# Cross-attention on one Trainium2 core: the softmax sum of half 0 taken from right sums of products 1 and 2, T1 of e and T4 of y made by ScalarE and transfers

## The chip, the core and the metric

The kernel runs on one core of a Trainium2 chip. The core's engines work side by side, each through its own list of instructions in order: TensorE (PE in the profile, its weight loads PEld) multiplies matrices out of the on-chip memory into accumulation banks; VectorE (DVE), ScalarE (ACT) and GpSimd (POOL) work element by element; SyncE (SP) issues plain transfers. GpSimd also issues transfers, among them those that add what they bring to what already stands at the destination. The engines wait for each other by semaphores.

The metric is the device time of one execution in microseconds (us). Unless another unit is named, all times below are us.

## The reference

Eight batches, each with a query source x1 and a context x2 of 512 channels by 1024 positions:

```python
B, C1, C2, N = (8, 512, 512, 1024)          # D = C2 // 8 = 64
q = jnp.einsum('bcn,dc->bnd', x1, Wq) + bq
k = jnp.einsum('bcn,dc->bdn', x2, Wk) + bk[:, None]
v = jnp.einsum('bcn,dc->bdn', x2, Wv) + bv[:, None]
attn = jax.nn.softmax(jnp.einsum('bnd,bdm->bnm', q, k), axis=2)
attn_out = jnp.einsum('bcm,bnm->bcn', v, attn)
return attn_out + x1
```

All of it is in 32-bit floats.

## The kernel before, in words

**Order of the mathematics.** For each batch the kernel computes scores with keys on the partitions and queries along the free dimension, subtracts each query's maximum, and takes exponentials: this is e. Then it multiplies the context itself with e (y = x2 · e), divides y by the sum of the exponentials over the keys, and only then applies Wv, the bias and x1 (o = Wv · y + bv + x1).

**Halves and blocks.** Queries are taken in two halves h = 0 and 1 of H = 512 columns; keys in two halves of four tiles of 128 (MH = 4). So e is a 2 x 2 matrix of blocks: "11" and "21" are the two key halves for queries of half 0, "12" and "22" those of half 1. x2 (called a) and Wv (called w) are 2 x 2 blocks too.

**Seven products.** Both multiplications use a scheme of seven block products instead of eight. For y its right sums are T1 = e12 − e11, T2 = T1 + e22, T3 = e22 + e12 and T4 = T2 − e21 with its sign turned where the code says so; its left sums are S1 to S4 of a. Most of the seven products of y are split in the same way once more: `left_stream` and `right_stream` make the inner S and T sums of product i (tiles aI and eI with the product's number), `multiply_seeded` runs the inner products in the order 1, 7, 6, 2, 5, 4, 3. There, ScalarE copies a partial result out of a running chain of accumulation (L746) while TensorE works on something else, and TensorE then goes on in the same chain. The products of o use `multiply_41` (with y's product 4), `multiply` and `multiply_57`; their T1, T2 and T4 of y are made in `sum_y`.

**Periods.** `period(s, n, nn, nnn)` runs once per batch. It holds the products of y and o of batch s, and beside them the scores, maxima, exponentials and first sums of batch n, the next one; nn and nnn are those behind it. The order of all instructions on every engine is the order in which the functions are called: nothing reorders them. `s.six` holds for batches 2 to 5, `five` is true in the periods of batches 1 to 6. Batch 0, batch 1 and the last one have branches of their own.

**Queues.** ScalarE's list holds in one order the exponentials (L331), the copies of the scores (L245), the copies out of the chains (L746, L849), evictions of outputs (L930) and copies with the sign turned (L165, L177, L355). POOL's list holds the reductions across partitions (maximum L272, sum L291) and the issues of all transfers that add: x1 into outputs (L942, L900), a's sums (L160, L169, L181), T3 of e (L366, e22 into e12), T4 of e (L361), and tiles of e into the softmax sum (`add_tile`, L966). These transfers share one queue and move in its order. Plain loads and the outputs go by SP's queue.

**The softmax sum of half 0 of batch n.** In period s: `first_sum` copies tile 0 of e to a tile of sums (ScalarE, L971) and adds tile 1 by a transfer; tiles 2 and 3 are added by two more transfers, each issued when its exponential is made (`add_exponential`, `add_tile`). At the end of the period `total` adds the two key halves on VectorE (L266), and `reduce_total` adds across partitions on POOL and moves the result to a small tile of 128 x 4 (`few`). `invert` takes the reciprocals and writes them to a row in DRAM; `spread` broadcasts that row. For half 1 the sum comes from T3 (`sum_1`), since T3 is e12 + e22.

**T1, T2, T3 of e of batch n.** After its last exponential, `open_t` names the tiles, VectorE makes T1 (L340, two instructions, one for each pair of tiles), and two transfers make T3 in the place of e12. At the start of the next period, behind product 1, VectorE makes T2 = T1 + e22 (L340 again). Product 6 needs T2, product 5 needs T1 (its inner right sums are `sums_5`, L537 eI5), products 7 and 3 come behind.

**T4 of y** is y21 − T2, made by VectorE (L429), read by the last product of o in the period (`second(4)`, L464 ps_oc<-yT,w).

Of the kernel before, what the change touches and what calls it, by code (L numbers as in the profile page):

```python
# [15 lines left out]
def kernel(  # L16
# [48 lines left out]
    P = 128  # L65
# [211 lines left out]

    def sum_1(s):

        t = s.t["T3"]  # L280
        s.mx[1] = sb.tile([P, 2, H], F32, tag="fold", name=f"sum_{s.b}_1", bufs=2)
        nc.vector.tensor_tensor(s.mx[1], t[:, 0:2, :], t[:, 2:4, :], ALU.add)
        fold_halves(s, 1, ALU.add)
# [53 lines left out]
    def right_sums(t, k):  # L337

        x, y = {"T1": ("12", "11"), "T2": ("T1", "22"), "T3": ("22", "12")}[k]
        nc.vector.tensor_tensor(t[k], t[x], t[y], ALU.subtract if k == "T1" else ALU.add)  # L340
# [173 lines left out]

    def left_stream(s, i, x, tag):

        v = {f"{p + 1}{q + 1}": x[:, ts(q, MH // 2), ts(p, P)] for p in range(2) for q in range(2)}
        sums = sb.tile([P, 4, MH // 2, P], F32, tag=tag, name=f"aI{i}_{s.b}")
        s.inner[i] = v
        for z, (k, x, y, op) in enumerate(LEFT):  # L520
            v[k] = sums[:, z]
            nc.vector.tensor_tensor(v[k], v[x], v[y], op)  # L522
            yield
# [4 lines left out]
    def right_stream(s, i, x, *tags):  # L528
# [5 lines left out]
        sums = [sb.tile(shape, F32, tag=t, name=f"eI{i}{t}_{s.b}") for t in tags]  # L534
        both, t2, t4 = sums[0][:, 0:2], sums[-1][:, last - 2], sums[-1][:, last - 1]
# [577 lines left out]
    def period(s, n, nn, nnn):  # L1113
# [42 lines left out]
        def add_exponential(i):  # L1156
            exponential(n, 0, i)
            add_tile(n, 0, i)

        def while_11(j):  # L1160
            if five and j == 0 and nn:
                add_exponential(3)

        def while_57(j):
            if nn:
                exponential(n, 1, j)
            elif j == 0:
                add_exponential(3)
            else:
                exponential(n, 1, 0)  # L1170
# [4 lines left out]

        def first_sum():
            copy_first(n, 0)
            add_tile(n, 0, 1)
# [56 lines left out]
        else:  # L1235
# [3 lines left out]
            sum_e(s, *(("T2",) if early else ("T1", "T2")))  # L1239
# [14 lines left out]
            if n and not early:  # L1254
                invert(s, 0)
            if s.b > 1:
# [103 lines left out]
        if n:  # L1360
# [15 lines left out]
            elif nn:  # L1376
                first_sum()
# [28 lines left out]
        if five:  # L1406
# [4 lines left out]
            next(products, None)  # L1411
            if s.six:
                exponential(n, 0, 2)
            if nn is None:
                first_sum()
# [13 lines left out]
        scale_y(s, "21")  # L1429
        if n is None:  # L1430
# [28 lines left out]
        if s.six:  # L1459
            add_tile(n, 0, 2)  # L1460
        elif five:
            add_exponential(2)
# [13 lines left out]
        if n:  # L1476
            if five:
                sums_1 = left_stream(n, 1, n.a["11"], "i2")
                next(sums_1)
                weave(sums_1, singly(lambda: lower(n, 1, 2), lambda: sum_y(s, "T4")))  # L1480
# [38 lines left out]
        if n:  # L1519
# [14 lines left out]
            total(n, 0)  # L1534
# [46 lines left out]
```

## Time and profile before

| | us |
|---|---|
| median of 3 runs | 665.4 (664.44 to 666.31) |
| span of the profiled execution, first to last instruction | 662.5 |
| TensorE busy in it | 657.7 |
| VectorE busy | 622.4 |
| ScalarE busy | 379.7 |
| GpSimd busy | 225.5 |
| share of the 16 transfer engines taken by POOL's queue, SP's queue | 50.4%, 30.6% |

The profiled execution is one execution on the chip; of it the profile gives the span and not the time of the whole execution, which takes in what lies ahead of the first and behind the last instruction. The granted clock of TensorE is 1.000 over the span.

In a timeline, a line gives the start, the duration, the engine, the source line, the operation, out<-in by the program's names, the shapes, and how many instructions are merged; in brackets stands how long the engine had been idle and what ended it. Matmuls overlap: one of 128x256 lasts 0.38 in the records, though the next starts 0.216 after it. Each matmul of the source is two instructions in the trace. A line of transfer issues gives the size of one transfer and the time from issue to landing. A line of a queue gives packets, MB, and the share of the engines' time in the stretch that was asked for.

### The profile page before, as it was taken

Reading aid. Unit: us, or ns where it says so; the run is one execution under the profiler, and the core shown is the slowest. Engines: PE = TensorE matmul, PEld = TensorE weight load, DVE = VectorE, ACT = ScalarE, POOL = GpSimd, SP = SyncE. Lnnn points to the kernel's source line nnn. Section 1 sums busy time; section 2 is a strip of 40 time slices with the busy share of each in tenths; the row PEclk is TensorE's granted clock in tenths of the full one; section 3 lists DMA queues with packets and bytes.
Section 4 is the critical chain, followed back from the end, with each engine's and each line's share of the span. In section 5 each row is a group of like instructions: output and inputs, shape, how many; then the busy total and the mean of one; then the engine's idle time right before and its main releaser. Section 6 shows DMA issues by size and latency. Waiting matters only on the chain.

```text
span 662.5 us, 7988 instructions
## 1 busy us (share of the span) xinstructions
PE 657.7 (99%) x2626; PEld 433.7 (65%) x2626; DVE 622.4 (94%) x869; ACT 379.7 (57%) x728; POOL 225.5 (34%) x192
## 2 busy tenths in 40 slices
PE   9999999999999999999999999999999999999997
PEld 4435755756658666677666686576865757666865
DVE  1999999999999998999989999899999989999997
ACT  3755557446475575665756647656576555574332
POOL 0125215631255412463126431364213640244300
PEclk9999999999999999999999999999999999999999
DMA  8688578994899859998599995998948994399604
GB/s 329 259 281 255 118 256 147 210 261 142 276 162 227 240 164 299 194 245 198 166 290 204 227 232 148 276 209 203 273 91 192 216 243 176 77 180 242 132 15 152
DMA packets 51545, 135.88 MB, mean 205 GB/s; under 512 B 5680, under 2 KB 6192, under 8 KB 51504
## 3 DMA queue, kind: packets, MB, share of 16 engines
q0 software_dynamic: 24512, 61.94, 50.4%
q1 hardware_dynamic: 26848, 73.29, 30.6%
q8 instruction: 21, 0.34, 0.2%
q10 hardware_dynamic: 144, 0.14, 0.1%
q14 instruction: 20, 0.16, 0.1%
HBM read 87.83 MB, written 16.81 MB: 158 GB/s over the span
## 4 chain that ended last, share of the span: by engine, by line
PE 98%; DMA 1%; SPq 0%; DVE 0%; issue 0%
PE ps_yc L555 9%; PE ps_ya L555 7%; PE ps_oc L464 7%; PE ps_oa L689 7%; PE ps_s L236 6%; PE ps_ya L464 4%; PE ps_oa L464 4%; PE ps_q L191 4%; PE ps_i5chain L555 3%; PE ps_i4b L840 3%; PE ps_k L191 3%; PE ps_i3chain L555 3%; PE ps_i7chain L555 3%; PE ps_oc L840 3%; PE ps_i1chain L555 3%; PE ps_i2chain L555 3%
## 5 line engine op out<-in xcount | busy, mean ns | idle before, releaser
L331 ACT ACTIVATE e<-e 128x1024 f32<-128x1024 f32 x60 | 63.4, 1059 | 25.6 <-DVE e L322 25.2
L291 POOL PARTITION_ALL_REDUCE den<-sum x16 | 52.8, 3298 | 59.0 <-DVE sum L266 54.2
L322 DVE TENSOR_TENSOR e<-e,top 128x1024 f32<-128x1024 f32 x60 | 72.3, 1217 | 0.2 <-POOL top L272 0.2
L272 POOL PARTITION_ALL_REDUCE top<-max x16 | 31.4, 1960 | 94.1 <-DVE max L266 68.1
L966 POOL DMA_DIRECT2D sum<-e x21 | 25.9, 1235 | 82.0 <-ACT sum L971 32.6
L245 ACT COPY e<-ps_s 128x512 f32<-128x512 f32 x90 | 47.8, 622 | 10.1 <-PE ps_s L236 7.6
L236 PE MATMUL ps_s<-q,k 64*128 64x512 f32 (+1 forms) x188 | 46.6, 598 | 0.0
L256 DVE TENSOR_TENSOR max<-max,e 128x1024 f32<-128x1024 f32 x30 | 36.6, 1218 | 0.3
L236 PEld LDWEIGHTS ps_s<-q,k 64*128 64x128 f32 x188 | 17.5, 186 | 19.9 <-issue 17.4
L875 DVE TENSOR_TENSOR y<-y,den 128x1024 f32<-128x1024 f32 x24 | 29.2, 1220 | 0.3
L522 DVE TENSOR_TENSOR aI<-a,aI 128x256 f32<-128x256 f32 x60 | 28.1, 468 | 0.9
L746 ACT COPY ps_yc<-ps_i7chain 128x256 f32<-128x256 f32 x32 | 11.4, 357 | 30.2 <-PE ps_i7chain L555 26.1
L689 PE MATMUL ps_oa<-yT,w_S 128*128 128x512 f32 x56 | 27.4, 592 | 0.0
L307 POOL DMA_DIRECT2D den<-row x12 | 6.7, 558 | 59.0 <-DMA row<-few 47.8
L522 DVE TENSOR_TENSOR aI<-a 128x256 f32<-128x256 f32 x60 | 26.3, 464 | 0.0
L689 PE MATMUL ps_oa<-y,w_S 128*128 128x512 f32 x56 | 26.3, 592 | 0.0
L191 PE MATMUL ps_q<-x_in_x_dram,wqk_sb 128*64 128x512 f32 x112 | 25.6, 598 | 0.0
L746 ACT COPY ps_ya<-ps_i5chain 128x256 f32<-128x256 f32 x32 | 11.5, 361 | 24.2 <-PE ps_i5chain L555 20.0
L464 PE MATMUL ps_oa<-yT,w_S 128*128 128x512 f32 x56 | 25.2, 593 | 0.0
L464 PE MATMUL ps_oc<-yT,w 128*128 128x512 f32 x56 | 25.2, 592 | 0.0
L555 PE MATMUL ps_yc<-e,aI 128*128 128x256 f32 x92 | 23.6, 379 | 0.0
L746 ACT COPY ps_ya<-ps_i1chain 128x256 f32<-128x256 f32 x28 | 10.0, 357 | 22.1 <-PE ps_i1chain L555 18.5
(346 smaller groups left out, 1840.0 us busy)
## 6 DMA issues: line engine op xcount, KB each, us to landing
x_in_x_dram<-in_x_dram SPq DMA_DIRECT2D x60, 512.0 KB, 7.9
a<-in_x2T_dram SPq DMA_DIRECT2D x32, 512.0 KB, 7.0
aS<-in_x2T_dram POOLq DMA_DIRECT2D x21, 512.0 KB, 10.2
sum<-e POOLq DMA_DIRECT2D x21, 512.0 KB, 6.2
eT<-eT POOLq DMA_DIRECT2D x16, 512.0 KB, 11.9
r<-in_x_dram POOLq DMA_DIRECT2D x14, 512.0 KB, 8.3
uo<-in_x_dram POOLq DMA_DIRECT2D x14, 512.0 KB, 9.8
out_dram<-r SPq DMA_DIRECT2D x14, 512.0 KB, 8.9
```

Source lines behind the costliest of these rows:

```text
L191: nc.tensor.matmul(ps[r, :], w_sb[:, c, :], s.x[:, c, ts(h, H)], start=(c == 0), stop=(c == CT - 1),)
L236: nc.tensor.matmul(ps[g][:, n], s.k[r, ts(i, P)], s.q[r, ts(h, H)][:, n], start=True, stop=True)
L245: nc.scalar.copy(e[:, g, i, :], ps[g])
L256: nc.vector.tensor_tensor(f, e[:, :, 0, :] if i == 1 else f, e[:, :, i, :], op)
L291: nc.gpsimd.partition_all_reduce(s.den[h], s.mx[h][:, 0, :], P, ReduceOp.add)
L322: nc.vector.tensor_tensor(e, e, top, ALU.subtract)
L331: nc.scalar.activation(e, e, AF.Exp)
L464: nc.tensor.matmul(ps, left[ka][:, k, ts(j, P)], right[kb][:, k, :], start=opens and k == 0, stop=i in (2, 3, 4) and k == n_k - 1, skip_gr ...
L522: nc.vector.tensor_tensor(v[k], v[x], v[y], op)
L555: nc.tensor.matmul(ps, s.inner[i][ka][:, k, :], s.inner[i, "t"][kb][:, k, :], start=opens and k == 0, stop=z in (2, 3, 4) and k == n_k - 1 ...
L689: nc.tensor.matmul(ps, w[ka][:, k, ts(j, P)], s.y[kb][:, k, :], start=False, stop=i == 3 and k == 1, skip_group_check=True,)
L840: nc.tensor.matmul(ps, s.inner[i][ka][:, k, :], s.inner[i, "t"][kb][:, k, :], start=opens and k == 0, stop=z in (2, 3, 4) and k == n_k - 1 ...
```

## The change

Three edits, with what follows from them in the order of calls.

1. **Half-0 sum of batches 2 to 7.** The copy and the three transfers of the sum are dropped; the exponentials keep their places. The inner right sums of products 1 and 2 are made with another set of signs, so that their T3 is e22 + e12 of the inner blocks and T4 + T3 is e21 + e11; the left sums of these two products turn sign to match (`LEFT_SUM`). In `right_stream` a single 128x1024 instruction for T1 and T3 becomes two of 128x512. `total_0` adds the pairs T4, T3 of both products in one 128x1024 instruction, whose output is laid out so that after the reduction a small tile of 64 x 8 holds, for every four queries, both parts. `invert` adds the parts for the left queries before the reciprocal.
2. **T1 of e, batches 2 to 5.** VectorE no longer makes T1. ScalarE writes −e22 to its tile in two halves (`begin_t1`, behind the issues of T3). In the next period VectorE makes T2 as T3 − e11, and two transfers add T2 to the tile of T1 (`end_t1`, ahead of S4's transfer on POOL).
3. **T4 of y, in the periods of batches 1 to 5.** ScalarE writes −T2 to its tile behind the copies of `multiply_41` (`copy_yt4`), and a transfer adds y21 to it once that is scaled. The VectorE instruction is dropped.

```diff
+    def total_0(s):
+        s.mx[0] = f = sb.tile([P, 2, H], F32, tag="fold", name=f"sum_{s.b}_0", bufs=2)
+        x, y = (s.inner[i, "m"].rearrange("q z k (p f) -> q z k p f", p=D) for i in (1, 2))
+        nc.vector.tensor_tensor(f.rearrange("q k (p z f) -> q z k p f", p=D, z=2), x, y, ALU.add)
+        fold_halves(s, 0, ALU.add)
+        s.den[0] = sb.tile([P, H], F32, tag="den", name=f"den_{s.b}_0", bufs=2)
+        nc.gpsimd.partition_all_reduce(s.den[0], f[:, 0, :], P, ReduceOp.add)
+        s.few[0] = sb.tile([D, 2, H // P], F32, tag="fews", name=f"fews_{s.b}", bufs=2)
+        nc.gpsimd.dma_start(
+            s.few[0].rearrange("p z f -> p (z f)"), s.den[0][0:1, :].rearrange("o (p f) -> o p f", p=D)
+        )
...
     def invert(s, h):
-        nc.vector.reciprocal(s.few[h], s.few[h])
+        few = s.few[h]
         s.row[h] = row = dram.tile([1, H], F32, tag="row", name=f"row_{s.b}_{h}")
-        nc.gpsimd.dma_start(row.rearrange("o (p f) -> (o p) f", p=P), s.few[h])
+        to = row.rearrange("o (p f) -> (o p) f", p=P)
+        if h == 0 and s.b > 1:
+            nc.vector.tensor_tensor(few[:, 0, :], few[:, 0, :], few[:, 1, :], ALU.add)
+            to = row.rearrange("o (z p f) -> (o p) z f", z=2, p=D)
+        nc.vector.reciprocal(few, few)
+        nc.gpsimd.dma_start(to, few)
...
+            "T2 of T3": ("T3", "11", ALU.subtract),
...
+    def begin_t1(s):
+        for i in (0, 2):
+            nc.scalar.mul(s.t["T1"][:, i : i + 2, :], s.t["22"][:, i : i + 2, :], -1.0)
+
+    def end_t1(s):
+        for i in (0, 2):
+            nc.gpsimd.dma_start(
+                s.t["T1"][:, i : i + 2, :], s.t["T2"][:, i : i + 2, :], accum_op=ALU.add
+            )
...
+    def copy_yt4(s):
+        nc.scalar.mul(s.y["T4"], s.y["T2"], -1.0)
...
-        for z, (k, x, y, op) in enumerate(LEFT):
+        for z, (k, x, y, op) in enumerate(LEFT_SUM if i in (1, 2) else LEFT):
...
+        if i in (1, 2):
+            for z, k in enumerate(("T1", "T2", "T4", "T3")):
+                v[k] = sums[z // last][:, z % last]
+            s.inner[i, "t"], s.inner[i, "m"] = v, sums[-1][:, last - 2 : last]
+            for k, x, y, op in (
+                ("T1", "12", "11", ALU.subtract),
+                ("T3", "22", "12", ALU.add),
+                ("T2", "T1", "22", ALU.add),
+                ("T4", "21", "T2", ALU.subtract),
+            ):
+                nc.vector.tensor_tensor(v[k], v[x], v[y], op)
+                yield
+            return
...
         def while_11(j):
             if five and j == 0 and nn:
-                add_exponential(3)
+                exponential(n, 0, 3)
...
-            sum_e(s, *(("T2",) if early else ("T1", "T2")))
+            sum_e(s, *(("T2 of T3",) if s.six else ("T2",) if early else ("T1", "T2")))
...
+            if s.six:
+                end_t1(s)
             if s.b > 1:
                 add_s4(s)
...
-            elif nn:
-                first_sum()
...
+            if nn:
+                copy_yt4(s)
             if s.six:
                 exponential(n, 0, 2)
...
         scale_y(s, "21")
+        if five and nn:
+            nc.gpsimd.dma_start(s.y["T4"], s.y["21"], accum_op=ALU.add)
...
-        if s.six:
-            add_tile(n, 0, 2)
-        elif five:
-            add_exponential(2)
+        if five and not s.six:
+            exponential(n, 0, 2)
...
             if nn:
-                sum_e(n, "T1")
+                if not n.six:
+                    sum_e(n, "T1")
                 sum_t3(n, 0)
                 sum_t3(n, 2)
+                if n.six:
+                    begin_t1(n)
...
-            total(n, 0)
+            if five:
+                total_0(n)
+            else:
+                total(n, 0)
```

More of the change, by code (lines that the diff above doesn't have):

```diff
@@ L337, in right_sums @@
     def right_sums(t, k):
-        x, y = {"T1": ("12", "11"), "T2": ("T1", "22"), "T3": ("22", "12")}[k]
-        nc.vector.tensor_tensor(t[k], t[x], t[y], ALU.subtract if k == "T1" else ALU.add)
+        x, y, op = {
+            "T1": ("12", "11", ALU.subtract),
+            "T2": ("T1", "22", ALU.add),
+            "T3": ("22", "12", ALU.add),
+            "T2 of T3": ("T3", "11", ALU.subtract),
+        }[k]
+        nc.vector.tensor_tensor(t[k[:2]], t[x], t[y], op)
     def open_t(s):
@@ L513, in in_turn @@
             yield from stream
+    LEFT_SUM = (
+        ("S3", "21", "11", ALU.subtract),
+        ("S1", "21", "22", ALU.subtract),
+        ("S2", "11", "S1", ALU.subtract),
+        ("S4", "12", "S2", ALU.subtract),
+    )
     def left_stream(s, i, x, tag):
@@ L1154, in scores_0 @@
             return then
-        def add_exponential(i):
-            exponential(n, 0, i)
-            add_tile(n, 0, i)
         def while_11(j):
             if five and j == 0 and nn:
-                add_exponential(3)
+                exponential(n, 0, 3)
         def while_57(j):
@@ L1167, in while_57 @@
             elif j == 0:
-                add_exponential(3)
+                exponential(n, 0, 3)
             else:
@@ L1174, in early_s2 @@
             add_11(n, "S2")
-        def first_sum():
-            copy_first(n, 0)
-            add_tile(n, 0, 1)
         if not s.t:
@@ L1414, in period @@
             if nn is None:
-                first_sum()
                 begin_s1(n)
@@ L1479, in period @@
                 next(sums_1)
-                weave(sums_1, singly(lambda: lower(n, 1, 2), lambda: sum_y(s, "T4")))
+                weave(
+                    sums_1, singly(lambda: lower(n, 1, 2), *([] if nn else [lambda: sum_y(s, "T4")]))
+                )
         if n is None:
```

## The prediction

> **What bounds the kernel now.** I read the busy times on the first page, then the waits of TensorE, then the order of time around the places that the change touches.
>
> ```profile
> PE 657.7 (99%) x2626; PEld 433.7 (65%) x2626; DVE 622.4 (94%) x869; ACT 379.7 (57%) x728; POOL 225.5 (34%) x192
> ```
>
> All waits of TensorE in the trace are two, both in the head:
>
> ```profile
> PE ps_warm L1029 <- DVE warm L1026: 1.0, 1, 1.0
> PE ps_ka L1003 <- DMA x_head<-in_x2h_dram: 0.3, 1, 0.3
> ```
>
> The span is TensorE's own work, matmul behind matmul, and the change touches no matmul. VectorE, which it relieves in some batches, is 94% busy and still never late by a wait that shows. So time saved on VectorE has nothing to shorten; what can change the time is a hand-off to TensorE that comes later than now. The rest is a search for those, in a period of the middle batches (here the change from batch 2 to batch 3; batches 2 to 5 have the same order).
>
> **ScalarE at the start of a batch.** ScalarE gets the two copies that begin T1 (−"22", 128x1024 each). They stand in its queue behind the last exponential, and ahead of the eviction of output "12" (L930), the negation for S3 (L177) and the copies of product 1. The rows of ScalarE, of TensorE beside it, and of the VectorE instruction that releases the exponential:
>
> ```profile
> 272.09 1.22 DVE L322 TENSOR_TENSOR e<-e,top 128x1024 f32<-128x1024 f32 x1
> 273.34 1.06 ACT L331 ACTIVATE e<-e 128x1024 f32<-128x1024 f32 x1 [1.59 <-DVE e L322]
> 274.31 1.25 ACT L930 ACTIVATE r<-ps_oa,wqk_sb 128x512 f32<-128x512 f32 x2
> 275.44 1.05 ACT L177 ACTIVATE a<-a 128x1024 f32<-128x1024 f32 x1
> 276.57 1.03 PE L555 MATMUL ps_i1chain<-e,a 128*128 128x256 f32 x4
> 277.69 0.36 ACT L746 COPY ps_ya<-ps_i1chain 128x256 f32<-128x256 f32 x1 [1.20 <-PE ps_i1chain L555]
> 278.30 1.03 PE L555 MATMUL ps_i1chain<-eI1yT,aI 128*128 128x256 f32 x4
> ```
>
> From 273.34 to 274.31 an instruction of this size holds ScalarE for 0.97, so two take about 1.9. The exponential can't start earlier (its VectorE instruction keeps its place, 272.09, behind an eviction of TensorE's). So L930 moves to 276.2, L177 to 277.35, and the copy of the chain, 0.97 behind that, to 278.3; now it starts at 277.69, after 1.20 idle. It ends at 278.67. TensorE adds to that same chain at 278.30, so it has to wait for the copy's end. How soon it follows is seen where such a copy is already late, in batch 6:
>
> ```profile
> 541.86 0.47 ACT L746 COPY ps_ya<-ps_i5chain 128x256 f32<-128x256 f32 x1
> 542.39 1.13 PE L555 MATMUL ps_i5chain<-eI5u,aI 128*128 128x256 f32 x4
> ```
>
> Copy over at 542.33, matmul at 542.39: 0.06. The new start is 278.75, 0.45 late. Four batches (2 to 5): **+1.8**. Bounds: nothing, if the two copies together take under 1.45; 1.0 each, if a copy waits besides.
>
> The copy for T4 of y lies elsewhere on ScalarE, before the exponential of tile 2:
>
> ```profile
> 256.08 1.08 ACT L331 ACTIVATE e<-e 128x1024 f32<-128x1024 f32 x1
> 258.34 0.58 ACT L475 COPY uo<-ps_oa 128x512 f32<-128x512 f32 x1 [1.18 <-PE ps_oa L464]
> ```
>
> There 1.18 idle time covers its 0.97; without that cover it would delay an eviction that has a whole product of TensorE before its bank is used again. Cost 0. Its transfer starts once y "21" is scaled, and product 4 reads it:
>
> ```profile
> 258.28 1.22 DVE L875 TENSOR_TENSOR y<-y,den 128x1024 f32<-128x1024 f32 x1
> 273.14 3.60 PE L464 MATMUL ps_oc<-yT,w 128*128 128x512 f32 x8
> sum<-e POOLq DMA_DIRECT2D x1, 512.0 KB, 9.2
> ```
>
> From 259.5 on, a transfer that takes as long as the sum's transfer now at that place (9.2) lands at 268.7; 4.4 are left. Cost 0.
>
> **VectorE.** Rows of the old T1 (two of 128x1024) and of what follows:
>
> ```profile
> 273.23 2.43 DVE L340 TENSOR_TENSOR eT<-e,e 128x1024 f32<-128x1024 f32 x2
> 275.57 0.68 DVE L542 TENSOR_TENSOR eI1yT<-eI1yT,e 128x512 f32<-128x512 f32 x1
> 276.18 0.42 DVE L522 TENSOR_TENSOR aI<-a 128x256 f32<-128x256 f32 x1
> ```
>
> Start to start, 128x1024 takes 1.17 and 128x512 0.61. Where products 1 and 2 now split one 128x1024 into two 128x512, each pays 0.05 more: 0.1 a batch. [...]
>
> The new half-0 sum adds one 128x1024 (in sixteen-byte runs, which no row shows: between 1.17 and twice that; I take 1.17, the row of the same size and type). In batches 2 to 5 it takes the place of two such instructions for T1 and VectorE reaches the sum no later. In batch 6, 1.3 more is swallowed by this pause of VectorE:
>
> ```profile
> 540.20 1.23 DVE L256 TENSOR_TENSOR max<-e 128x1024 f32<-128x1024 f32 x1 [1.64 <-ACT e L245]
> ```
>
> In **batch 7** nothing of it is given back, 1.17 + 0.1 + some 0.1 for the larger reciprocal, together 1.4, and VectorE runs without a pause until past product 7. Two hand-offs there:
>
> ```profile
> 615.62 1.58 DVE L537 TENSOR_TENSOR eI7yT<-e 128x1024 f32<-128x1024 f32 x1
> 618.32 1.03 PE L555 MATMUL ps_i7third<-eI7yT,aI 128*128 128x256 f32 x4
> 628.99 1.29 DVE L891 TENSOR_TENSOR y<-ps_ya,uy 128x512 f32<-128x512 f32 x2
> 631.27 0.59 PE L840 MATMUL ps_oa<-eIo1i,w_I 128*128 128x256 f32 x2
> ```
>
> The first leaves 1.12 (617.20 to 618.32), the second 0.99 (630.28 to 631.27). With 1.4 the larger loss counts: **+0.4**. Bounds 0 to 1.6 (the sum at twice its price).
>
> **The transfers of T1.** T2 now comes from T3, which a transfer makes, and T1 needs two more transfers after T2. Now:
>
> ```profile
> 267.85 1.19 POOL L966 DMA_DIRECT2D sum<-e  x1 [5.74 <-ACT ps_oc L564]
> 275.00 1.81 POOL L366 DMA_DIRECT2D e<-e  x2 [2.05 <-issue]
> e<-e POOLq DMA_DIRECT2D x1, 512.0 KB, 10.1
> 282.98 2.71 DVE L340 TENSOR_TENSOR eT<-eT,e 128x1024 f32<-128x1024 f32 x2
> 285.35 1.25 POOL L942 DMA_DIRECT2D r<-in_x_dram  x1
> r<-in_x_dram POOLq DMA_DIRECT2D x1, 512.0 KB, 8.8
> 295.36 1.22 DVE L537 TENSOR_TENSOR eI5aI<-eT 128x1024 f32<-128x1024 f32 x1
> ```
>
> The second half of T3, issued near 275.95, lands near 286.05; T2's second half starts near 284.5. With today's queue T2 would wait 1.6. But the sum's transfer at 267.85, for which POOL had stood 5.74 with everything behind it, is gone, and the queue is shorter by its 0.52 MB. The rate, in a stretch with POOL's queue alone and one with outputs beside it:
>
> ```profile
> q0 software_dynamic: 229, 0.47, 107.1%
> q0 software_dynamic: 115, 0.41, 83.2%
> q1 hardware_dynamic: 104, 0.21, 25.3%
> ```
>
> 0.47 MB in 2.4 us (0.196 per us) alone, 0.41 MB in 2.5 us (0.164) with 0.21 MB of outputs. So the queue runs 2.7 earlier, T3 lands at 283.4 and T2 waits for nothing. T1's 1.05 MB stand behind the output's transfer r, which now lands at 285.35 + 8.8 = 294.1: less 2.7, plus 6.4, gives T1 at 298.1. VectorE wants it at 295.36 and so waits 2.75. It gives back 0.45 and 0.35 in two pauses before it meets the next narrow place:
>
> ```profile
> 307.89 0.70 DVE L763 TENSOR_TENSOR ps_ya<-ps_ya,v 128x512 f32<-128x512 f32 x1 [0.45 <-ACT ps_ya L746]
> 313.93 0.70 DVE L763 TENSOR_TENSOR ps_yc<-ps_yc,v 128x512 f32<-128x512 f32 x1 [0.35 <-ACT ps_yc L746]
> 316.40 0.60 ACT L863 ACTIVATE uy<-ps_yc 128x512 f32<-128x512 f32 x1
> 317.05 0.36 ACT L746 COPY ps_yc<-ps_i3chain 128x256 f32<-128x256 f32 x1
> 317.66 0.59 PE L555 MATMUL ps_i3chain<-eI3eT,aI 128*128 128x256 f32 x2
> ```
>
> The addition at 313.93 moves by 1.95 and ends at 316.58. ScalarE's copy at 316.40 reads its result; with TensorE 0.45 late already it is due at 316.85, and 0.19 more is free before the chain's copy (over at 317.41) holds the matmul at 317.66. That leaves 0.4. So **0** is my value, and T1 landing after 298.5 costs TensorE what it exceeds. If the queue is no earlier than now, T1 comes at 300.5 and each of four batches loses 2.0 more (the wait for T2 is then inside this one). S4's transfer, queued on POOL behind T1's, has several us until product 3's sums; the half-0 sum's small transfers keep their size.
>
> [...]
>
> **The sum.** 1.8 + 0.4 + 0 = 2.2 on the profiled span of 662.5, so 664.7. The median of the runs, 665.4, is 2.9 above that span, which I add: **667.6**.
>
> **Rivals.**
> *T1 lands late.* A wait of VectorE for T1's second half replaces the sums it was spared, and TensorE pays in product 3. For it: 0.4 of room beside an estimate of queue times; against it: the freed 0.52 MB. From 298.5 on. At 300.5: 2.2 + 4 x 2.0 = 10.2, so 675.6; half of that, 671.6.
> *Not slower.* The two copies of T1 hold ScalarE for under 1.45 together, so that the chain's copy is in time at 278.30. Then only batch 7's 0.4 is left: 665.8. For it: 1.59 idle just before; against it: 0.97 for every instruction of this size here, and the idle time lies ahead of an exponential that waits for VectorE.
> *A gain.* A freer VectorE and queue close waits. All that TensorE waits for is 1.3, in the head, out of reach; at the very most 664.1.
> *The relief turns on itself.* The strided half-0 sum costs twice the row: 1.6 in batch 7 and the rest as forecast, 668.8.
>
> **How the numbers follow.** A measurement here tells 0.3%, 2.0 us, from no change: same is 663.4 to 667.4. Forecast 0.45, of its own range 666.6 to 669 (a third falls under 667.4); T1 late 0.25; not slower 0.22; the costly sum 0.05; a gain 0.03. Slower: 0.30 + 0.25 + 0.05 = 0.60; same 0.15 + 0.22 = 0.37; faster 0.03. The range runs from 665.0, which leaves out the gain and some of the not-slower cases, to 675.0, which takes in nearly all of a late T1.
>
> **What would show it.** In batches 2 to 5 the copy out of product 1's chain follows L177 with no idle time, and the next matmul on that chain starts some 0.45 late. A wait of VectorE for T1's transfer of 2 to 3 stands ahead of product 5's right sums. If it is over 3.2, TensorE is late in product 3. T2 doesn't wait for T3. In batch 7 the third of product 7 starts about 0.3 late. The forecast is wrong if TensorE's matmuls run on without these gaps, if a gap stands elsewhere (product 6, the scores, product 4 of the output), or if the sum of gaps is over 4.

## The result, and the profile after

| | before | changed |
|---|---|---|
| median of 4 runs each, on one chip | 665.86 (664.44 to 667.44) | 672.82 (670.82 to 674.4) |
| ratio, with its 95% interval | | 1.0107 (1.0084 to 1.0129) |
| span of the profiled execution | 662.5 | 670.2 |
| time of that execution | | 671.95 |
| granted clock of TensorE in it | 1.000 | 1.000 |

The change costs 7.0 by the medians and 7.7 by the spans. The busy times of the changed kernel's page:

```profile
PE 660.9 (99%) x2626; PEld 432.9 (65%) x2626; DVE 617.0 (92%) x882; ACT 386.5 (58%) x735; POOL 216.0 (32%) x187
```

Its waits (engine, tile and line that waited, what it waited for; total, times, longest), three of TensorE's and one of VectorE's:

```profile
PE ps_i3chain L613 <- ACT ps_yc L804: 3.0, 3, 1.1
PE ps_i1chain L613 <- ACT ps_ya L804: 1.0, 4, 0.3
PE ps_i7third L613 <- DVE eI7yT L595: 0.5, 1, 0.5
DVE eI5aI L595 <- DMA eT<-eT: 15.3, 4, 4.1
```

VectorE is 5.4 less busy, as meant, and TensorE has three kinds of waits that it did not have. A wait of TensorE in these rows is shorter than the delay (0.25 for 0.41 in product 1 below), since the end that the profile gives the matmul before it (279.83 + 1.03) reaches into the gap. So below a gap is the time by which a matmul starts later behind the one ahead of it than the same pair does without a wait (0.86 for four instructions of 128x256). When TensorE resumes after a gap, another 0.10 goes into the next pair of starts (281.11 to 282.07 there, 0.96 and not 0.86).

**Product 1** (timeline, the batch for which the prediction worked it out):

```profile
275.73 1.06 ACT L349 ACTIVATE e<-e 128x1024 f32<-128x1024 f32 x1 [1.59 <-DVE e L340]
276.70 1.99 ACT L389 ACTIVATE eT<-e 128x1024 f32<-128x1024 f32 x2
278.59 1.25 ACT L988 ACTIVATE r<-ps_oa,wqk_sb 128x512 f32<-128x512 f32 x2
279.73 1.05 ACT L177 ACTIVATE a<-a 128x1024 f32<-128x1024 f32 x1
279.83 1.03 PE L613 MATMUL ps_i1third<-eI1yT,aI 128*128 128x256 f32 x4
280.68 0.38 ACT L804 COPY ps_ya<-ps_i1chain 128x256 f32<-128x256 f32 x1
281.11 1.13 PE L613 MATMUL ps_i1chain<-eI1yT,aI 128*128 128x256 f32 x4 [0.25 <-ACT ps_ya L804]
```

The two copies hold ScalarE from 276.70 to 278.59, 1.89. No row behind them shows idle time, and the matmul follows the copy's end (281.06) by 0.05. It starts 1.28 behind the one ahead (279.83) and not 0.86, so the chain's matmuls come 0.41 to 0.42 late, in each of four batches, with the resumption 2.1 in all.

**T1 and product 3.** VectorE's right sums of product 5 in the four batches (2 to 5), then the path in product 3 of the batch with the shortest of these waits:

```profile
220.23 1.22 DVE L595 TENSOR_TENSOR eI5aI<-eT 128x1024 f32<-128x1024 f32 x1 [3.98 <-DMA eT<-eT]
301.48 1.23 DVE L595 TENSOR_TENSOR eI5aI<-eT 128x1024 f32<-128x1024 f32 x1 [3.23 <-DMA eT<-eT]
383.58 1.23 DVE L595 TENSOR_TENSOR eI5aI<-eT 128x1024 f32<-128x1024 f32 x1 [4.08 <-DMA eT<-eT]
465.62 1.23 DVE L595 TENSOR_TENSOR eI5aI<-eT 128x1024 f32<-128x1024 f32 x1 [4.03 <-DMA eT<-eT]
...
319.09 0.69 DVE L821 TENSOR_TENSOR ps_yc<-ps_yc,v 128x512 f32<-128x512 f32 x1
319.81 0.60 ACT L921 ACTIVATE uy<-ps_yc 128x512 f32<-128x512 f32 x1 [0.40 <-DVE ps_yc L821]
320.44 0.36 ACT L804 COPY ps_yc<-ps_i3chain 128x256 f32<-128x256 f32 x1
320.85 1.13 PE L613 MATMUL ps_i3chain<-eI3eT,aI 128*128 128x256 f32 x4
```

The matmul of 320.85 starts 0.50 behind the one ahead of it and not 0.22. In the four batches it comes 1.30, 0.28, 1.13 and 1.07 late, with the resumptions 4.2 in all. Of this 0.2 is not the change's: in the third of the four the same start came 0.08 late in the kernel before, with its resumption. That leaves 4.0. Three of the pairs agree on where it begins: 3.23 − 0.28, 4.08 − 1.13 and 4.03 − 1.07 lie at 2.95 or 2.96 (the first batch's, 3.98 − 1.30, at 2.7). In this execution VectorE may wait 2.95, and what is over it TensorE loses, us for us.

**Why T1 is late.** POOL in the first of these batches (batch 2):

```profile
201.80 3.23 POOL L285 PARTITION_ALL_REDUCE den<-sum  x1 [2.08 <-DVE sum L266]
205.89 1.26 POOL L1000 DMA_DIRECT2D r<-in_x_dram  x1
206.65 2.29 POOL L394 DMA_DIRECT2D eT<-eT  x2
```

The two queues in it from 208 to 210 (packets, MB, share of the 16 engines' time; q0 is POOL's queue, q1 SP's):

```profile
q1 hardware_dynamic: 414, 0.82, 106.9%
q0 software_dynamic: 4, 0.00, 0.2%
```

In batch 2 the adding queue did run earlier, and then it stood empty for over 2 us: all that was ahead had been moved, and r, its next transfer, is issued at 205.89, behind the half-0 reduction and the small transfer that waits for it. Its packets begin at 210.48. Meanwhile the plain outputs take the engines. Batch 5, with the wait of 4.03, has the same hole (from 454 to 455.9 the adding queue has 3 packets, 0.01 MB, and the plain outputs 0.70 MB). In batch 4, with 4.08, there is none, but outputs run beside r (0.25 MB from 373 to 375), which takes 8.2 from issue to landing as in batch 2. In batch 3, with 3.23, the queue is busy until r begins (109.4% from 288 to 290), and r takes 7.4.

An earlier hole stands in all four batches, 3.9 to 4.0 long, ahead of the transfers of S2 and T3. In batch 3, POOL, and all that the queues move from 274 to 277:

```profile
275.07 0.90 POOL L181 DMA_DIRECT2D aS<-in_x2T_dram  x1 [7.05 <-ACT aS L177]
...
q1 hardware_dynamic: 272, 0.52, 45.1%
```

There the adding queue moves no data from 273.74 to 277.69. In the kernel before it is full at that place (337 packets, 0.66 MB, 100.5% from 271 to 275). With the sum's transfers gone it has nothing to move until S2's transfer is issued, which waits for ScalarE's negation: much of the time that the change freed on the queue passes with the queue empty. How much of the lead is left further on, from issues and landings, counted from the start of product 1's first matmul in each batch (before / changed):

| | batch 2 | batch 3 | batch 4 | batch 5 |
|---|---|---|---|---|
| large transfer ahead of r (a, L181) lands | 15.7 / 11.7 | 14.5 / 13.0 | 14.3 / 12.8 | 14.1 / 11.5 |
| r is issued | 10.0 / 9.2 | 8.8 / 8.6 | 8.8 / 8.6 | 8.8 / 9.2 |
| r lands | 18.9 / 17.4 | 17.5 / 16.0 | 17.5 / 16.8 | 17.1 / 17.3 |
| T1's second half lands | – / 23.4 | – / 22.5 | – / 23.3 | – / 23.2 |

The queue ahead of r runs 1.5 to 4.0 earlier, r's issue 0.8 earlier at most, and r lands 1.5, 1.5 and 0.7 earlier and 0.2 later.

**The last batch**, of VectorE in the kernel before (two rows), and of VectorE and TensorE in the changed one:

```profile
590.22 1.22 DVE L537 TENSOR_TENSOR eI1yT<-e 128x1024 f32<-128x1024 f32 x1
596.36 0.69 DVE L266 TENSOR_TENSOR sum<-sum 128x512 f32<-128x512 f32 x1
```

```profile
597.01 0.68 DVE L590 TENSOR_TENSOR eI1yT<-e 128x512 f32<-128x512 f32 x1
602.68 0.69 DVE L590 TENSOR_TENSOR eI2eT<-e,eI2eT 128x512 f32<-128x512 f32 x1
603.41 1.23 DVE L282 TENSOR_TENSOR sum<-eI1yT,eI2eT 128x1024 f32<-128x1024 f32 x1
604.67 0.69 DVE L266 TENSOR_TENSOR sum<-sum 128x512 f32<-128x512 f32 x1
616.93 0.14 DVE L316 TENSOR_TENSOR fews<-fews 64x4 f32<-64x4 f32 x1
617.11 0.20 DVE L318 RECIPROCAL fews<-fews 64x8 f32<-64x8 f32 x1
624.12 1.59 DVE L595 TENSOR_TENSOR eI7yT<-e 128x1024 f32<-128x1024 f32 x1
625.76 1.13 PE L613 MATMUL ps_i7third<-eI7yT,aI 128*128 128x256 f32 x4 [0.48 <-DVE eI7yT L595]
```

From the first right sum of product 1 to that of product 7 (590.22 to 615.62 before, 597.01 to 624.12 now) VectorE needs 27.11 in place of 25.40 (615.62 is a row of the prediction): 1.71 more. It had 1.12 to spare, and product 7's third comes 0.65 late.

The gaps at these three kinds of places make 2.1 + 4.0 + 0.75, or 6.9; the other 0.8 of the 7.7 lies in starts up to 0.2 later at other hand-offs.

### The profile page after: what moved, and what is told of

It is laid out like the page before. It is cut to its first block, busy times and chain, and to the rows that moved or that the text cites. A ratio compares the mean times of both kernels' runs of the same rounds, so it can differ in the third digit from the quotient of the medians.

```text
span 670.2 us, 8006 instructions
## 1 busy us (share of the span) xinstructions
PE 660.9 (99%) x2626; PEld 432.9 (65%) x2626; DVE 617.0 (92%) x882; ACT 386.5 (58%) x735; POOL 216.0 (32%) x187
## 4 chain that ended last, share of the span: by engine, by line
PE 65%; DVE 19%; DMA 6%; issue 4%; ACT 3%; POOL 2%; DVEq 0%; POOLq 0%; ACTq 0%
DMA eT<-eT 6%; PE ps_yc L613 5%; PE ps_s L236 5%; PE ps_oa L747 5%; PE ps_oc L502 4%; DVE aI L567 4%; PE ps_oa L502 4%; PE ps_k L191 3%; PE ps_ya L502 3%; PE ps_ya L613 3%; PE ps_i4b L898 3%; DVE e L340 3%; DVE max L256 2%; PE ps_oc L898 2%; PE ps_q L191 2%
## 5 line engine op out<-in xcount | busy, mean ns | idle before, releaser
L236 PEld LDWEIGHTS ps_s<-q,k 64*128 64x128 f32 x188 | 17.4, 186 | 20.0 <-issue 17.4
L804 ACT COPY ps_ya<-ps_i5chain 128x256 f32<-128x256 f32 x32 | 11.5, 360 | 24.2 <-PE ps_i5chain L613 20.0
L567 DVE TENSOR_TENSOR aI<-a 128x256 f32<-128x256 f32 x60 | 24.9, 440 | 0.0
L1000 POOL DMA_DIRECT2D r<-in_x_dram x14 | 18.3, 1304 | 15.2 <-ACT r L988 14.5
## 6 DMA issues: line engine op xcount, KB each, us to landing
eT<-eT POOLq DMA_DIRECT2D x24, 512.0 KB, 11.7
```

The source lines that it names most:

```text
L236: nc.tensor.matmul(ps[g][:, n], s.k[r, ts(i, P)], s.q[r, ts(h, H)][:, n], start=True, stop=True)
```

## The experiments

Each result is the median of its runs and the ratio to the kernel before on the same chip, with its interval. "Before" was 664.84, 664.90 and 665.39 in the three sets of runs below (665.86 beside the first result), so between sets ratios are compared.

**T1 of e made by VectorE again** in batches 2 to 5; the new half-0 sum and T4 of y stay.

```diff
-            sum_e(s, *(("T2 of T3",) if s.six else ("T2",) if early else ("T1", "T2")))
+            sum_e(s, *(("T2",) if early else ("T1", "T2")))
...
-            if s.six:
-                end_t1(s)
...
-                if not n.six:
-                    sum_e(n, "T1")
+                sum_e(n, "T1")
...
-                if n.six:
-                    begin_t1(n)
```

> T1 of e by VectorE again in batches 2 to 5, T2 from T1; the new half-0 sum and the new T4 of y stay. If ScalarE's copies and the landing of T1 make the loss before batch 7, both kinds of gap go (product 1: 4 x 0.42; product 3: 3.8 together) and batch 7's 0.65 to 0.9 stays: 5.5 to 6.5 under the changed kernel, within 0.3% of before plus 1. If the new sum or the new T4 of y cost in the middle batches too, it stays 3 or more above before, with gaps of TensorE somewhere in batches 2 to 6.

Measured: 668.37, 1.0046 (1.0031 to 1.0060). Its waits of TensorE, beside those at the start and product 7's:

```profile
PE ps_k L449 <- DMA x_in_x_dram<-in_x_dram: 1.0, 2, 0.8
PE ps_i2chain L613 <- ACT ps_yc L804: 0.5, 1, 0.5
```

All waits in products 1 and 3 are gone, and about half of the loss with them (4.1 by the ratios, where 5.5 to 6.5 was expected). The rest is larger than expected. Product 7's wait stays. A wait in product 2 of batch 2 is new (a gap of 0.68, and smaller ones of 0.13 in products 2 and 6 later): now VectorE has both T1 and the sum's 1.23, which is more than it had before. So the sum does cost in the middle batches, as the rival said, where T1 is left on VectorE; in the changed kernel no such gap stands there. And a load of x in the head comes late, ahead of all that the edit touches. Seven of the thirteen profiled executions here have that wait, and six, the changed kernel's two among them, don't.

**Product 5's left sums, and product 4's, ahead of its right sums,** so that VectorE works while T1 is on its way.

```diff
             if s.six:
-                weave(*sums_5)
+                weave(sums_5[0])
+                inner_left(s, 4, s.a["22"], "a12")
+                weave(sums_5[1])
```

(The later call of `inner_left` for product 4 is dropped.)

> Only VectorE's order changes: in batches 2 to 5 the left sums of products 5 and 4 (2.8 us that need no T1) run ahead of the right sums of product 5. T1 lands as late as before. If VectorE's wait for T1 is what makes TensorE late in product 3, the wait shrinks from 3.2 to 4.1 to about 0.5 to 1.3, the gaps of 0.3 to 1.3 in product 3 are gone, and the time falls by about 4. If they come from ScalarE's own load or from transfers beside, they stay and the time is the changed kernel's.

Measured: 668.02, 1.0046 (1.0030 to 1.0063). VectorE's wait for T1:

```profile
DVE eI5aI L595 <- DMA eT<-eT: 6.3, 4, 2.3
```

VectorE's wait falls from 15.3 to 6.3, no wait in product 3 is left, and product 1's stays as it was. So the wait for T1 is what TensorE loses in product 3.

**Half of T1's copy ahead of the last exponential,** in ScalarE's idle 1.59.

```diff
         if five:
+            open_t(n)
+            if n.six:
+                begin_t1(n, 0)
             exponentials(n, 1, 3)
...
                 if n.six:
-                    begin_t1(n)
+                    begin_t1(n, 2)
```

> Only ScalarE's order changes: the first half of T1's copy moves ahead of the last exponential, into ScalarE's idle time. Both theories: the gap of 0.42 in product 1 of batches 2 to 5 goes. If the two delays add, the time falls by 1.7 to 2.1. If T1's landing is set by the transfers' queue alone, TensorE reaches product 3 that much earlier and waits that much longer there: the gaps of product 3 grow by about 0.4 each and the time hardly falls (0 to 0.5).

Measured: 673.05, 1.0122 (1.0105 to 1.0139).

```profile
PE ps_i3chain L613 <- ACT ps_yc L804: 3.2, 4, 1.2
PE ps_i3chain L613 <- DVE aI L567: 1.6, 2, 0.8
DVE eI5aI L595 <- DMA eT<-eT: 16.2, 4, 5.2
```

Product 1's wait is gone and the time did not fall. What TensorE gained in product 1 it lost in product 3. T1 landed no earlier for it: counted from product 1's first matmul, at 23.1 in the mean of the four batches, as in the changed kernel.

**Both of these edits together.**

> Both orders together (left sums of products 5 and 4 ahead, first half of T1's copy ahead of the last exponential). If the two kinds of gap and batch 7's are all there is, batches 2 to 5 have no gap left in products 1 and 3, 6 of the 7.7 come back, and the time is about 0.9 above before. If something else is lost, it shows here as a rest of over 1.5 above before.

Measured: 666.89, 1.0024 (1.0014 to 1.0034).

```profile
DVE eI5aI L595 <- DMA eT<-eT: 5.1, 4, 2.1
```

No wait is left in products 1 and 3. With T1's wait filled, the early copy is worth 1.0046 − 1.0024, 1.5 of its 2.1 (1.7 by the spans, 666.2 and 664.5; the two intervals overlap a little). The same edit was worth nothing ahead of a late transfer (1.0122 beside 1.0107) and most of its size where the wait for that transfer was filled with other work.

**The last batch's half-0 sum made the old way,** alone, and then with the two edits above (all three).

```diff
-        if h == 0 and s.b > 1:
+        if h == 0 and 1 < s.b < B - 1:
...
             if nn is None:
+                copy_first(n, 0)
+                add_tile(n, 0, 1)
                 begin_s1(n)
...
-            if five:
+            if five and nn:
                 total_0(n)
```

(Tiles 2 and 3 are added by `add_tile` behind their exponentials, as before.)

> The changed kernel with the half-0 sum of the last batch alone made the old way (a copy by ScalarE, three transfers that add, the sum of the two key halves on VectorE); all else as changed. Theory: the new sum puts about 1.7 of VectorE's time ahead of product 7 of the last batch, where 1.1 was free, so TensorE's gap of 0.65 at product 7's third goes and nothing else does: about 0.7 to 1.0 less than the changed kernel, and the gaps in products 1 and 3 of batches 2 to 5 stay. Rival: the gap at product 7 comes from something else of the change; then it stays and the time is that of the changed kernel.

Measured: 673.13, 1.0127 (1.0111 to 1.0142). This missed. The waits:

```profile
PE ps_i3chain L613 <- ACT ps_yc L804: 3.6, 4, 1.2
DVE eI5aI L595 <- DMA eT<-eT: 17.4, 4, 5.0
```

Product 7's wait is no longer among them, but VectorE waited 2.1 longer in all for T1 than in the changed kernel's profile, in batches that the edit does not touch. T1's landings differ that much between executions (in batch 3 by 1.5 between the changed kernel's two profiles, 22.5 and 24.0 in the table below), and a late load of x in the head adds 0.9 in this one, so nothing below 1 can be read beside them.

> The changed kernel with all three mends: the left sums of products 5 and 4 of e ahead of product 5's right sums, the first half of T1's copy ahead of the last exponential, and the last batch's half-0 sum made the old way. Theory: the three causes (ScalarE's copies ahead of product 1's chain, T1's late landing, the sum in the last batch) are all there is, but for some tenths in the head: span 663 to 664, ratio to the kernel before 1.000 to 1.002. Rival: the change has a cost that none of the three takes away; ratio 1.003 or more, with gaps at places not yet seen. A gain (under 0.998) is expected by neither, since TensorE has no waits to give back.

Measured: 665.48, 1.0008 (0.9999 to 1.0016). With T1's wait out of the way the same edit takes the ratio from 1.0024 to 1.0008: 1.1 for the last batch, with intervals that just meet; the gap itself was 0.75. The three causes are all there is, within what can be told.

**r's transfer ahead of the half-0 reduction on POOL.**

```diff
-            n.leave = [last] if five else [leave, last]
+            n.leave = [] if five else [leave, last]
             second(4)
             if five:
+                last()
                 total_0(n)
```

> The changed kernel with one issue moved: on POOL, x1's transfer to output 12 (r) ahead of the half-0 reduction across partitions, not behind it. All else as changed. Theory: in batches 2, 4 and 5 the queue that adds stands empty for some 2 us because r is issued only after the reduction (3.2) and its small transfer; with r ahead of them T1 lands 1.5 to 2 earlier, VectorE's waits for T1 shrink from about 4 to about 2 each, and TensorE's gaps in product 3 from 1.1 each to 0.3 or less: 2.5 to 4 less than the changed kernel. The gaps of 0.4 in product 1 stay. Rival: the outputs beside set the pace of T1's transfers; then r lands earlier, T1 doesn't, and the time falls by less than 1. Another way to fail: the reduction now stands behind r's wait for output 12, so the sum comes later and something behind it is late.

Measured: 670.33, 1.0080 (1.0066 to 1.0094). POOL and VectorE in the same batch as above:

```profile
200.10 1.58 POOL L1000 DMA_DIRECT2D r<-in_x_dram  x1
202.54 3.23 POOL L285 PARTITION_ALL_REDUCE den<-sum  x1 [0.86 <-DVE sum L266]
206.63 1.82 POOL L394 DMA_DIRECT2D eT<-eT  x2
...
218.93 1.22 DVE L595 TENSOR_TENSOR eI5aI<-eT 128x1024 f32<-128x1024 f32 x1 [1.94 <-DMA eT<-eT]
```

The adding queue from 208 to 210:

```profile
q0 software_dynamic: 172, 0.39, 104.8%
```

VectorE's waits for T1 in all four batches:

```profile
DVE eI5aI L595 <- DMA eT<-eT: 10.4, 4, 2.9
```

In that stretch, empty before, the adding queue now moves 0.39 MB. Counted from the reduction's start, T1 is there after 16.39 (218.93 − 202.54) and not after 18.43 (220.23 − 201.80): 2.0 earlier, though it is issued only 0.8 earlier. Counted from product 1's first matmul, T1 lands at 21.4, 22.2, 22.1 and 21.9: 2.0, 0.3, 1.2 and 1.3 earlier, least in batch 3, where nothing stood empty ahead of r. (The expectation counted such a hole in batch 4 too; there is none.) VectorE's longest wait is 2.9, under the 2.95 of above, and TensorE waits for nothing in product 3. The span is 3.2 shorter than the changed kernel's, though a late load of x in the head takes 1.5 of it. This execution was the fastest of its four (668.74); the others may still wait in product 3. Of the medians the ratio falls by 0.0027 beside the first result and by 0.0045 beside the repeat below (1.8 and 3.0).

**T4 of y alone,** in the kernel before: `copy_yt4` and its transfer, nothing else of the change.

> The kernel before with the third edit alone: T4 of y as a copy by ScalarE with the sign turned and a transfer that adds y21, in the periods of batches 1 to 5. VectorE is spared five instructions of 1.2. Theory: it costs nothing and brings nothing, since the copy lies in idle time of ScalarE and the transfer lands several us before product 4 of the output reads it: ratio 0.9985 to 1.0015. Rival: the copy delays an exponential or an eviction, or the transfer delays those that stand behind it in the queue (the sum's tiles, T3 of e): small gaps of 0.1 to 0.3 each in five periods, ratio 1.002 or more.

Measured: 664.72, 1.0001 (0.9992 to 1.0010). It costs nothing and, though it spares VectorE five instructions, brings nothing.

**r's transfer and the early copy together; the same with the last batch's old sum; the changed kernel again,** all on one chip.

> The changed kernel with two mends: r's transfer to output 12 ahead of the half-0 reduction on POOL, and the first half of T1's copy on ScalarE ahead of the last exponential. Theory: the copy moved alone brought nothing because T1's landing, not product 1's chain, set when product 3 could go on; with T1 in time the copy is worth its gaps in product 1, 0.41 and 0.10 in each of four batches: about 2 less than with r's transfer moved alone (ratio 1.004 to 1.006 beside 1.008). Rival: TensorE runs 0.5 earlier in each batch and so meets T1's transfers sooner; a gap in product 3 takes the place of the one in product 1, and the time stays near 1.008.

Measured: 669.97, 1.0070 (1.0056 to 1.0084).

```profile
PE ps_i3chain L613 <- ACT ps_yc L804: 2.0, 3, 1.0
DVE eI5aI L595 <- DMA eT<-eT: 12.7, 4, 3.3
```

Here the rival was right. TensorE gains 0.5 in product 1 and reaches product 3 that much earlier, so less of VectorE's wait is covered: waits of 2.8 to 3.3 now cost TensorE 0.3 to 1.2 each. They also grow, from 10.4 to 12.7 in all. Of these 2.3, VectorE's being ready earlier makes 0.5 (0.0 to 0.2 a batch, counted from product 1's first matmul), and T1's landing 1.4 later in batch 2 most of the rest. r's transfer brings T1 just in time for a late TensorE, with no room beyond.

> As the run before (r's transfer ahead of the reduction, T1's copy split around the last exponential), and the last batch's half-0 sum the old way. Theory: that sum is worth its gap at product 7 of the last batch, 0.65 and 0.24 behind it: 0.7 to 1.0 less than the run before, as 1.0024 fell to 1.0008 with product 5's right sums filled; ratio 1.003 to 1.005. The earlier run that undid this sum alone missed it because T1's landings, which differ from run to run by one to two us, covered it. Rival: the sum of the last batch costs nothing and the earlier fall was chance; then the two runs agree within 0.3.

Measured: 668.23, 1.0041 (1.0025 to 1.0057), 1.7 less than the run before and so more than its gap. Product 7's wait is gone; the fall holds less waiting in product 3 (1.6 beside 2.0) and for a load of x in the head too (none beside 0.9), both of which differ between executions. The 1.1 from the pair without T1's wait is the better figure.

> The changed kernel, nothing edited, beside the two runs above on one chip, so that their differences to it don't cross chips. Theory: 1.0095 to 1.013, with a wait of VectorE for T1 of 3 to 5 in each of batches 2 to 5 and gaps in product 3 wherever that wait is over 3.2. Rival: the earlier time was that chip's; then 1.008 or less, and r's transfer would have less to win than was read from it.

Measured: 674.06, 1.0125 (1.0106 to 1.0144).

```profile
DVE eI5aI L595 <- DMA eT<-eT: 15.8, 4, 4.9
DVE eT L363 <- DMA e<-e: 1.3, 1, 1.3
```

The loss repeats, with T1 late by as much. But not in the same way everywhere. In batch 5 the adding queue does not run empty ahead of r; outputs move beside r and T1 instead, and T1 lands 7.6 behind r and not 5.9. In one batch T2 waited for T3's transfer too, 1.3, the only execution looked at in which it did by over 0.3. No version is faster than the kernel before: the best two agree with it.

**What T1's landing goes with.** In the traces of the changed kernel, its repeat and the run with r's transfer moved, the MB of SP's queue from 8 us after product 1's first matmul until T1's second half lands, and that landing, counted from the same matmul:

| | batch 2 | batch 3 | batch 4 | batch 5 |
|---|---|---|---|---|
| changed | 1.19, 23.4 | 0.67, 22.5 | 1.07, 23.3 | 1.18, 23.2 |
| repeat | 1.31, 23.9 | 0.71, 24.0 | 0.55, 22.4 | 1.28, 24.0 |
| r's transfer moved | 0.59, 21.4 | 0.61, 22.2 | 0.67, 22.1 | 0.67, 21.9 |

With one exception T1 is latest where another 0.5 MB of plain outputs, one transfer, went ahead of its end. The exception is the batch in which T2 waited 1.3. That output goes ahead in the hole or beside r, and with r issued early it doesn't in any of the four. This is a comparison of traces; no run held an output back.

## Why the prediction was right or wrong

The median of 672.82 lies in the range, on the side forecast, and 5.2 over the time given. It is the case of a late T1, given a chance of 0.25, that came, at about the price it was given for half of its worst (671.6). The likeliest case did not, and by the prediction's own sign, gaps of over 4 in all, its forecast of 667.6 was wrong: they make 6.9.

**Right: ScalarE's copies.** The two hold ScalarE for 1.89 (1.9 predicted), the chain's copy stands 0.95 behind L177 (0.97), the matmul 0.05 behind the copy (0.06): 0.45 late predicted, 0.41 measured in each batch, 2.1 with the resumption for 1.8. The rival in which the copies fit into the idle time is ruled out by the rows: ScalarE has none behind them.

**Right: the path from T1 to TensorE.** Addition, ScalarE's eviction, the chain's copy, the matmul in product 3: each instruction stands in the rows as named, and no other place of the four batches is late through it. The room was given as 298.5 − 295.36 = 3.14 of waiting and is 2.95.

**Wrong: when T1 lands.** A wait of 2.75 was forecast; in the profiled execution it was 3.83 on average (15.3 / 4). A slip first: the prediction's own terms, 294.1 − 2.7 + 6.4, give 297.8 and not 298.1, so a wait of 2.45. Its 0 for TensorE doesn't change by that. The step that failed is "less 2.7" in the sum for T1: with the queue shorter by the sum's transfer, r and T1 would be 2.7 earlier. r was 1.5, 1.5 and 0.7 earlier and 0.2 later. The lead was not kept, since the queue ran empty: in all four batches ahead of S2's transfer, in two of them again ahead of r; of the 1.5 to 4.0 that the transfer ahead of r was early, 1.5 at most was left when r landed. POOL issues r behind the reduction of the sum, and the reduction waits for VectorE, which was hardly earlier (r's issue by 0.8 at most). What is ahead of a transfer in its queue was counted, and what is ahead of its issue on the engine was not. Where that made a hole or put r beside outputs, the waits are 3.98 to 4.08; in the batch without either it is 3.23. Issuing r ahead of the reduction takes the mean wait to 2.6 (10.4 / 4), nearly the forecast one, and leaves product 3 free of waits in the execution profiled. What the hole ahead of S2's transfer costs was not tried. The term "6.4" for T1's own two transfers held in the first execution, where they landed 5.9 to 6.5 behind r; in the repeat it was 6.5 to 7.6. Cost of this step: 4.0 of the 5.5 by which the sum on the span was short (664.7 beside 670.2).

**Wrong in size: the last batch.** 0.4 predicted, 0.65 measured in product 7, 0.75 with the resumption and 1.1 by the pair of experiments. VectorE needs 1.71 more and not 1.4. The sum's addition takes 1.26 to the next start, as its row of nearest size had said to 0.09 (the sixteen-byte runs cost nothing that shows: it lasts 1.23, L537's 128x1024 of 590.22 1.22; so the case of a costly sum is ruled out). The splits and the sum's own start took 0.26 (590.22 to 596.36 before, 597.01 to 603.41 now), 0.1 predicted: a split cost 0.06 and 0.08, and 0.12 more passes between the last of them and `total_0` (602.68 to 603.41), which reads what the instruction just ahead of it writes. The trace bears that out: VectorE's 128x512 additions and subtractions outside the accumulation banks are followed at once by another such instruction 181 times. 128 of the followers don't read the tile just written, and each starts 0.60 or 0.61 behind; the 33 that start over 0.67 behind all read it. The sum's own 1.26, ahead of an addition that reads it, beside 1.13 or 1.14 for most others of its size, is the same. The addition of the two parts (L316), 0.18 to the reciprocal, was not in the sum at all.

A split costs 0.06 and 0.08 and no more because two such instructions overlap at their ends: each lasts 0.68, and the next starts 0.60 or 0.61 behind, so for a row of independent ones the distance of starts decides, not the duration.

**Right: nothing for T4 of y** (1.0001 alone) **and, but for one batch of one execution, nothing for T2.**

**Wrong: 2.9 outside the span.** The changed kernel's execution of 671.95 has a span of 670.2, so 1.75 lies outside, and in all executions on record it is 1.7 to 2.0. So the span of 662.5 belonged to an execution of 664.2 to 664.5, the fastest of the three shown (664.44). Of the 2.9, about 1 is scatter between executions. It made the forecast larger by that much, and by luck brought it nearer to what was measured.

**The rival's own sum** added T1's loss to product 1's (2.2 + 4 x 2.0). The runs with the early copy show that they are not independent: without the stall in product 1 the ratio was 1.0122, beside 1.0107 with it, and TensorE waited longer in product 3 (3.2 + 1.6 beside 3.0), so the stall had given T1's transfer that time. The threshold of 298.5 had that in it, since it took TensorE 0.45 late, but then undoing the stall can't bring its 1.8 back as long as T1 is at the threshold.

What stays open is why an output goes ahead of T1 in one batch or execution and not in another (the same batch's landings differ by up to 1.5 between the changed kernel's two profiles, and waits of 3.23 and 4.86 stand in one execution), and the late loads of x in the head, which come and go.

## What to carry to other kernels

With work taken off the queue of transfers, the queue was earlier only as far as the issues were (r landed 1.5 earlier at most, where 2.7 was counted on): follow each transfer back to its issue, and each issue to what stands ahead of it on the issuing engine, here a reduction that waits for a third engine, and a negation on ScalarE. In the kernel before, whose TensorE has no waits behind the head, a busy VectorE had nothing to give (1.0001 with five of its instructions less), and each hand-off that is moved to another engine needs its room worked out first. Where two stalls follow each other in one batch, mend the later one first or both together: mending the earlier alone brought nothing (1.0122 beside 1.0107), and 1.5 of its 2.1 with the later one mended.

## What the runs showed of the hardware

**In these stretches beside outputs the two queues moved about as many packets each, not the same bytes or time.** The two queues from 214 to 216 in the kernel with r's transfer moved, while T1 is on its way beside outputs:

```profile
q0 software_dynamic: 92, 0.32, 79.1%
q1 hardware_dynamic: 93, 0.19, 27.8%
```

Packets are 92 and 93, and the adding queue has 0.16 MB per us, not much less than the 0.196 that it moves alone. An adding packet of T1 is larger (0.32 MB in 92, beside 0.19 in 93) and keeps an engine longer (79.1% for 92, beside 27.8% for 93), so that three quarters of the time are its own. The stretch from which the prediction has 0.164 is of this kind, with 115 packets and 104. These are counts of single stretches; from 210 to 212 in the changed kernel there are 126 and 98. Where the packets were of one size, the adding queue had fewer bytes: in the repeat of the changed kernel, from 456 to 458, with r beside outputs,

```profile
q0 software_dynamic: 128, 0.26, 70.4%
q1 hardware_dynamic: 128, 0.26, 39.2%
```

it has 0.13 MB per us.

**While the adding queue was empty, outputs went ahead.** Alone, plain outputs move 0.82 MB in 2 us (208 to 210 above), twice what the adding queue moved in the same stretch with r ahead. With r ahead none of their packets runs in that stretch, and they follow from 212 to 218 (0.16, 0.19 and 0.16 MB in 2 us each); T1 lands 2.0 earlier in that batch. Filling the hole is not all, though: batch 5 of the repeat has none, and T1 was as late there with outputs beside it.

**From an issue to its first packet** 4.6 and 4.4 pass for r behind the two holes (205.89 to 210.48, 451.49 to 455.84), and 2.6 to 3.3 for S2's transfer behind the four earlier ones (275.07 to 277.69 in batch 3). In the kernel before, S2's transfer is issued at 272.05 and the queue is full from 271 to 275 (100.5%), so that time is hidden there; to be hidden in the changed kernel too, these issues would have to come that much before the queue runs dry. What takes the time, and why it differs, the rows do not show.
